# Attention scores by seven products: two partial sums accumulated in PSUM, with another order of the products and a later sum of the second queries

## The chip, the cores and the metric

One core of a Trainium2 chip runs the kernel. The metric is the device time of one execution in microseconds (us). TensorE (PE) multiplies, with its weight loads (PEld) beside it; VectorE (DVE), ScalarE (ACT) and GpSimd (POOL) work on tiles; SyncE (SP) issues nearly all DMAs, in the order in which they stand in its queue. Every engine takes its instructions in order.

## The reference

A layer with attention and a gated low-rank feed-forward part on the same normalized input, 2 sequences of 2048 tokens, width 2048, head width 512. Cut to what matters here:

```python
xn = layernorm(x)
q, k, v = split(xn @ Wqkv + bqkv)                 # each (2, 2048, 512)
attn = softmax((q @ k.T) / sqrt(512))             # (2, 2048, 2048)
out = x + (attn @ v) @ Wo + bo + ffn(xn)
```

The change lies in `q @ k.T`.

## The kernel before

**Number format.** Each operand is split into a high and a low part (`split_hi` on ScalarE, line 121, and `split_lo` on VectorE, line 124). A product of two operands is then three matmuls (low x high, high x low, high x high: `PASSES`), all added up in one PSUM bank.

**Stages.** First the projections of blocks of 512 tokens. For the last three of the four block pairs they run in `phase`, seven phases of seven items (six features and "V"), each item's weights fetched two pieces ahead by `fetch` (DMA at line 605, then the splits). A feature item is 24 matmuls of 512 columns; the V item, in two pieces, has matmuls of 264 columns. Beside each phase `beside` gives a list of small steps to be done by the other engines: among them `key_list`, `query_steps`, `query_load` and `query_split`. Then come the scores with the weighted sums, then the output projection.

**Scores.** The tokens are NB = 8 blocks of 512; two neighbouring blocks b0 and b1 are a pair (four pairs, `NPAIR`). The scores of a pair with two key tiles are a 2 x 2 block product, computed with seven products P1 to P7 instead of eight. Their operands are sums of blocks, made beforehand: key sums by `key_steps` (written to `kp_d`, line 853, loaded by `key_load`, line 945), query sums by `query_steps` (loads at line 905, additions at 908 to 911, stores to `qs_d` at line 915) and loaded by `query_load` (928). For one pair there are NKS = 8 key positions m; a pair and a position are called a unit here, so there are 32 units with 7 products each, 224 products, numbered g. One product is six matmuls of 512 columns (two halves of the head width, three passes).

`score(g)` (line 1089 is its matmul) does one product in the order `ORDER` and hands its bank on. `acc()` gives one of seven PSUM banks. P1 stays in its bank and P2 is added there by TensorE; everything else is added in SBUF by VectorE:

```python
if step == "P1":
    nc.scalar.copy(unit(b0, m)[:, 1, :], ps)
if step == "P6":
    tt(u[:, 1, :], u[:, 1, :], ps, ALU.add)
elif step == "P5":
    tt(unit(b1, m)[:, 1, :], u[:, 1, :], ps, ALU.add)
```

P3, P7 (twice) and P4 are additions of the same kind, so a unit has two copies on ScalarE (lines 1096 and 1101) and six additions on VectorE (1099 to 1113). `greatest` (1071, 1073) keeps the running maximum of the scores of a block, in VectorE.

**After the scores of a block.** `maxes` turns the running maximum into one maximum for each query, a chain of some ten small VectorE operations that ends in `mq` (1132). `spread` sends it to all partitions by one matmul (1142), and ScalarE copies it to `mbc` (1146). `soft(c)` does a chunk of 128 keys: VectorE subtracts (1158), ScalarE takes the exponential (1161), then the split into `ph`. `weigh(n)` multiplies the chunk by the values (`vt`, loaded from `v_d` by `load_v`, 1185), line 129.

**Order.** The main loop goes over g. After `score(g)`, with every second g, it loads the keys of two products eight ahead into a ring of five double tiles (`r_kt`), does the steps that `deal` has put at g, and from product 65 on some `weigh` calls of the pair before. So the first pair's 56 products run one after another, and between the products of pairs 1 to 3 there are six to nine matmuls of weighted sums. `maxes` of the pair's second block is called at the product n = 54 of its 56, `spread` of it at n = 1 of the next pair; the first block's follow at n = 2 and 4. The framework orders each engine's instructions by its own estimate, near to the order in the program, and puts a semaphore wait at every dependency; a DMA also waits for the one eight before it.

The query sums of pair 1 (`query_steps(1, mid(0, 1, 2, 3))`) are steps of the last projection phase, P4 of the last pair, in two halves `l0, s0, o0` and `l1, s1, o1`: load, sums, store. Their loads write the four tiles of one ring twice. The operands of pair 1 are loaded and split at n from -14 and -6 on.

Of the kernel before, what the change touches and what calls it, by code (L numbers as in the profile page):

```python
# [8 lines left out]
F32 = mybir.dt.float32  # L9
FR = mybir.dt.float32r  # L10
# [6 lines left out]
P = 128  # L17
# [16 lines left out]
def raw(ap):  # L34
    return ap.bitcast(F32)
# [27 lines left out]
def attn_ffn_kernel(ctx: ExitStack, tc, x, xT, wq, wv, wob, bqk, bv, bo, keysT, out):  # L63
# [26 lines left out]
    def mid(*js):  # L90
        return Ring(sb, *(f"h{j}" for j in js))
# [41 lines left out]
    def scratch(name, n):  # L133
# [7 lines left out]
        [dram.tile([P, 2, 2, 2, P], F32, name=f"kp_d{kb}_{n}") for n in range(7)] for kb in range(NB)  # L141
# [518 lines left out]
    def beside(j, ph):  # L660
# [49 lines left out]
        if more:  # L710
# [6 lines left out]
        k, (l0, s0, o0, l1, s1, o1) = key_list(7, 8, False), query_steps(1, mid(0, 1, 2, 3))  # L717
        return [], [
            [ql(0), ql(1), l0], [qp(0), ql(2), *k[:2]], [s0, qp(1), ql(3), *k[2:4]],
            [o0, qp(2), ql(4), l1, k[4]], [qp(3), ql(5), *k[5:7]],  # L720
            [qp(4), ql(6), s1, k[7], kl(0), kl(1)], [o1, kl(2), kl(3), qp(5), qp(6)],
# [110 lines left out]
    ORDER = ("P1", "P6", "P2", "P5", "P3", "P7", "P4")  # L832
# [3 lines left out]
    qop, kop = {}, {}  # L836

    def key_steps(kb, d):


        v = {}

        def load():
            for h in range(2):
                v[h] = ks["R"]([P, T], F32, "kr")
                nc.sync.dma_start(v[h], k_d[kb][h][:, d, :])

        def quad(a, h):
            return v[h].rearrange("p (m a k) -> p a m k", m=2, a=2)[:, a]

        def out():
            if "out" in v:
                nc.sync.dma_start(*v.pop("out"))

        def one(step):
            a00, a01, a10, a11 = (quad(a, h) for a in range(2) for h in range(2))
            tt = nc.vector.tensor_tensor
            out()
            src = {"P1": a00, "P2": a01, "P4": a11, "P5": a11, "P7": a10, "P6": a00, "P3": a01}[step]
            if step == "P5":  # L860
                tt(a11, a10, a11, ALU.add)
            if step == "P7":
                tt(a10, a00, a10, ALU.subtract)
            if step == "P6":
                tt(a00, a11, a00, ALU.subtract)
            if step == "P3":
                tt(a01, a01, a00, ALU.subtract)
            n = steps.index(step)
            if ks["n"] == 1 or n % 2 == 0:
                v["st"] = ks["st"]([P, ks["n"], 2, 2, P], FR, "kst")  # L870
            st = v["st"][:, n % ks["n"]]
            split_hi(st[:, :, 0, :], src)
            split_lo(st[:, :, 1, :], src, st[:, :, 0, :])
            v["out"] = kp_d[kb][ORDER.index(step)][:, :, :, d, :], raw(st)

        steps = ("P1", "P2", "P4", "P5", "P7", "P6", "P3")
        return load, [lambda step=step: one(step) for step in steps] + [out]
# [43 lines left out]
    def query_load(j, n):  # L921

        h, t = {"P1": (0, 0), "P2": (1, 0), "P3": (1, 1)}.get(ORDER[n], (0, 0))
        src = q_d[2 * j + t][h]
        if ORDER[n] in ("P4", "P5", "P6", "P7"):
            src = qs_d[j][{"P5": 0, "P6": 1, "P7": 2, "P4": 3}[ORDER[n]]]
        hi, lo = (r_qt([P, 2, T], FR, "qt") for k in range(2))
        nc.sync.dma_start(raw(lo), src)
        qop[j, n] = hi, lo

    def query_split(j, n):
        hi, lo = qop[j, n]
        split_hi(hi, raw(lo))
        split_lo(lo, raw(lo), hi)

    def key_load(i):

        if 2 * i >= NPAIR * NKS * 7:
            return
        t = r_kt([P, 2, 2, 2, P], FR, "kt")  # L940
        for o in range(2):
            st, n = divmod(2 * i + o, 7)
            j, m = divmod(st, NKS)
            kb = j // 2 * BPB + m // 2
            last["sp"] = nc.sync.dma_start(raw(t[:, o]), kp_d[kb][n][:, m % 2])
            kop[2 * i + o] = t[:, o]
# [92 lines left out]
    ks = {"R": mid(0, 1, 2, 3), "st": wide(0, 1, 2, 3, 4, 5), "n": 2}  # L1039
# [26 lines left out]
    def greatest(blk, m, a):  # L1066
        u = S[blk, m]
        if m == 0:
            if a:
                M[blk] = r_M([P, T], F32, "M")  # L1070
                nc.vector.tensor_tensor(M[blk], u[:, 0, :], u[:, 1, :], ALU.max)
        else:
            nc.vector.tensor_tensor(M[blk], M[blk], u[:, a, :], ALU.max)  # L1073

    bank = {}

    def score(g):

        st, n = divmod(g, 7)
        j, m = divmod(st, NKS)  # L1080
        b0, b1 = 2 * j, 2 * j + 1
        step = ORDER[n]
        more = step == "P2"
        ps = bank["P1"] if more else acc()
        bank[step] = ps
        k, q = kop.pop(g), qop[j, n]
        for d in range(2):
            for i, (a, c) in enumerate(PASSES):
                last["pe"] = nc.tensor.matmul(  # L1089
                    ps, k[:, a, d, :], q[c][:, d, :],  # L1090
                    start=not more and d == 0 and i == 0, stop=d == 1 and i == 2,
                    skip_group_check=more,
                )
        tt = nc.vector.tensor_tensor
        if step == "P1":
            nc.scalar.copy(unit(b0, m)[:, 1, :], ps)
        u, v = S[b0, m], S.get((b1, m))
        if step == "P6":
            tt(u[:, 1, :], u[:, 1, :], ps, ALU.add)
        elif step == "P2":  # L1100
            nc.scalar.copy(u[:, 0, :], ps)
        elif step == "P5":
            tt(unit(b1, m)[:, 1, :], u[:, 1, :], ps, ALU.add)
            greatest(b0, m, 0)
        elif step == "P3":
            tt(v[:, 0, :], v[:, 1, :], ps, ALU.add)
            greatest(b1, m, 0)
        elif step == "P7":
            tt(v[:, 1, :], v[:, 1, :], ps, ALU.add)
            tt(u[:, 1, :], u[:, 1, :], ps, ALU.add)  # L1110
            greatest(b1, m, 1)
        elif step == "P4":
            tt(u[:, 1, :], u[:, 1, :], ps, ALU.add)
            greatest(b0, m, 1)
# [33 lines left out]

    blocks = [2 * j + t for j in range(NPAIR) for t in (1, 0)]
# [294 lines left out]

    deal(NG1 + 2, [small_ring])
# [10 lines left out]
    for j in range(1, NPAIR):  # L1456
        deal(NG1 * j - 14, [lambda j=j: query_load(j, 0), lambda j=j: query_split(j, 0)], 5)
        for n in range(1, 7):
            deal(
                NG1 * j - 7 + n, [lambda j=j, n=n: query_load(j, n), lambda j=j, n=n: query_split(j, n)],  # L1460
                5 if j == 1 else 3,
            )
# [3 lines left out]
    for g in range(begin[-1]):  # L1466
# [8 lines left out]
        if j and j <= NPAIR:  # L1475
            if n == 2:
                maxes(2 * j - 2)
            if n in (1, 4):
                with behind("pe"):
                    spread(2 * j - 1 - n // 4)  # L1480
        if n == NG1 - 2 and j < NPAIR:
            maxes(2 * j + 1)
# [118 lines left out]
```

## Time and profile before

| | us |
|---|---|
| median of three runs | 2637.76 (2636.66 to 2639.0) |
| the profiled execution | 2636.59 |
| its span | 2634.8 |
| score matmuls, line 1089, first to last start | 1336.6 to 1912.3 |
| VectorE, additions of line 1106, each of 32 | 0.681 |
| ScalarE, copies of line 1096, each of 32 | 0.587 |
| ScalarE, casts of queries, 128x1024, each of 28 | 1.051 |
| VectorE, subtractions of queries, 128x1024, each of 28 | 1.252 |
| VectorE, subtractions at line 1158, each of 64 | 1.214 |
| ScalarE, exponentials, each of 64 | 1.061 |
| key loads, 256 KB, issue to landing, median of 224 | 5.2 |
| stores of key sums, 256 KB, median of 112 | 3.7 |

How to read a profile of this kind: a row names the source line, the engine, the operation and the tiles (written <- read), then busy time and the mean of one. A row of waits says which engine stood idle, for which engine's or DMA's work, how long in total, how often and the longest. The granted clock is the share of full clock that TensorE had in a window. The queue of SyncE shows when each DMA was issued and how long the issue stood; a DMA that waits holds all behind it. An idle engine matters only where TensorE waits for it, since TensorE is busy nearly all the time.

### The profile page before, as it was taken

What the parts mean: (1) busy time and instruction counts of PE and PEld (TensorE: products, weight loads), DVE (VectorE), ACT (ScalarE), POOL (GpSimd) and SP (SyncE); (2) the same over time, 40 slices, a digit from 0 to 9 for tenths busy, and PEclk for the clock granted to TensorE, in tenths of its full rate; (3) what the DMA queues carried; (4) which work ended last, traced back from release to release, by engine and by line L of the source; (5) the groups of instructions that cost most, each with busy time, mean ns of one, the idle gap of its engine ahead of it and who ended that gap; (6) DMA issues with size and microseconds to landing.
All of it is one profiled execution on the core that took longest, in us unless ns stands there. A gap on an engine that the chain in (4) does not pass through costs nothing. (4 is left out here: it accounts for less than half of the span.)

```text
span 2634.8 us, 34738 instructions
## 1 busy us (share of the span) xinstructions
PE 2596.4 (99%) x12689; PEld 2193.7 (83%) x12689; DVE 1987.5 (75%) x2827; ACT 859.2 (33%) x1249; POOL 521.7 (20%) x315
## 2 busy tenths in 40 slices
PE   8999999999999999999989999999999999999999
PEld 7889888888888888888777887878877888888887
DVE  6557639867878677776678979979798776797675
ACT  4323323323332333343323434334254222332221
POOL 1311520000000010000000000000000666566654
PEclk9999999999999999999999999999999999999999
DMA  6677775668446673587999798899788544565542
GB/s 234 220 251 268 275 267 188 210 212 277 152 137 226 211 272 126 181 252 224 296 309 311 247 330 283 263 328 321 259 283 293 180 165 164 181 220 177 173 163 101
DMA packets 348042, 608.09 MB, mean 231 GB/s; under 512 B 28456, under 2 KB 151392, under 8 KB 347872
## 3 DMA queue, kind: packets, MB, share of 16 engines
q1 hardware_dynamic: 334912, 575.99, 64.9%
q10 hardware_dynamic: 12960, 29.89, 3.4%
q8 instruction: 100, 1.64, 0.3%
q14 instruction: 70, 0.57, 0.1%
HBM read 450.42 MB, written 155.35 MB: 230 GB/s over the span
## 5 line engine op out<-in xcount | busy, mean ns | idle before, releaser
L129 PE MATMUL acc<-t,pw 128*128 128x512 f32 x3024 | 694.0, 390 | 0.8 <-DVE pw L124 0.8
L129 PEld LDWEIGHTS acc<-t,pw 128*128 128x128 f32 x3024 | 565.4, 188 | 118.8 <-DVE pw L124 1.6
L1363 PE MATMUL acc<-wb,s 128*128 128x512 f32 x2688 | 609.8, 389 | 0.3 <-ACT u L1375 0.3
L1363 PEld LDWEIGHTS acc<-wb,s 128*128 128x128 f32 x2688 | 504.4, 188 | 105.5 <-ACT u L1375 0.8
L1347 POOL TENSOR_TENSOR xo<-xo,bo_bc 128x512 f32<-128x512 f32 x128 | 207.8, 1630 | 900.5 <-DMA bo_bc<-in_bo 601.7
L129 PE MATMUL acc<-ph,vt 128*128 128x512 f32 x1536 | 379.0, 391 | 4.8 <-ACT ph L121 3.0
L129 PEld LDWEIGHTS acc<-ph,vt 128*128 128x128 f32 x1536 | 289.0, 189 | 67.5 <-ACT ph L121 3.3
L1089 PE MATMUL acc<-qt,kt 128*128 128x512 f32 x1344 | 336.7, 393 | 3.5 <-DMA kt<-kp_d 1.8
L1089 PEld LDWEIGHTS acc<-qt,kt 128*128 128x128 f32 x1344 | 254.6, 190 | 59.2 <-DVE qt L124 2.7
L121 ACT CAST pw<-pw 128x1024 fp32r<-128x1024 f32 (+1 forms) x168 | 177.7, 1058 | 338.1 <-PE acc L129 245.1
L124 DVE TENSOR_TENSOR pw<-pw 128x1024 fp32r<-128x1024 f32 (+1 forms) x168 | 213.6, 1272 | 79.2 <-ACT pw L121 77.6
L129 PE MATMUL acc<-xh,wh 128*128 128x512 f32 x1152 | 263.6, 390 | 0.0
L129 PE MATMUL acc<-pw,t 128*128 128x264 f32 x2016 | 249.3, 285 | 10.7 <-ACT pw L121 9.9
L129 PEld LDWEIGHTS acc<-pw,t 128*128 128x128 f32 x2016 | 247.8, 189 | 13.1 <-ACT pw L121 10.3
L129 PEld LDWEIGHTS acc<-xh,wh 128*128 128x128 f32 x1152 | 215.6, 188 | 44.9
L121 ACT CAST s<-xz 128x1024 fp32r<-128x1024 f32 x112 | 118.0, 1054 | 368.7 <-PE acc L1363 307.5
L124 DVE TENSOR_TENSOR s<-xz,s 128x1024 fp32r<-128x1024 f32 x112 | 173.1, 1548 | 40.1 <-ACT s L121 40.1
L124 DVE TENSOR_TENSOR wh<-wu,wh 128x512 fp32r<-128x512 f32 x96 | 80.9, 860 | 101.5 <-ACT wh L121 101.5
L518 POOL TENSOR_TENSOR zt<-zt,g 128x512 f32<-128x512 f32 x24 | 41.4, 1732 | 510.5 <-DMA g<-gd 312.3
L1352 DVE TENSOR_TENSOR xo<-xo,acc 128x512 f32<-128x512 f32 x128 | 86.8, 680 | 54.7 <-POOL xo L1393 24.0
L121 ACT CAST ph<-sp 128x512 fp32r<-128x512 f32 x128 | 78.8, 617 | 141.7 <-PE acc L129 136.2
L124 DVE TENSOR_TENSOR t<-xq,t 128x1024 fp32r<-128x1024 f32 x84 | 108.3, 1293 | 21.0 <-ACT t L121 20.5
(165 smaller groups left out, 2512.8 us busy)
## 6 DMA issues: line engine op xcount, KB each, us to landing
vt<-v_d SPq DMA_DIRECT2D x128, 512.0 KB, 4.9
kt<-kp_d SPq DMA_DIRECT2D x224, 256.0 KB, 5.2
pw<-sq_d SPq DMA_DIRECT2D x72, 512.0 KB, 4.1
xo<-in_x SPq DMA_DIRECT2D x128, 256.0 KB, 3.2
xz<-oz_d SPq DMA_DIRECT2D x64, 512.0 KB, 4.5
out_y<-xo SPq DMA_DIRECT2D x128, 256.0 KB, 2.6
kp_d<-kst SPq DMA_DIRECT2D x112, 256.0 KB, 3.7
pw<-in_wq SPq DMA_DIRECT2D x54, 512.0 KB, 4.2
```

What stands on the lines that cost most here:

```text
L121: return nc.scalar.copy(hi, src)
L124: return (eng or nc.vector).tensor_tensor(lo, src, raw(hi), ALU.subtract)
L129: last["pe"] = nc.tensor.matmul(ps, st(a_), mv(b_), start=first and n == 0, stop=end and n == 2)
L518: nc.gpsimd.tensor_tensor(zt, zt, gx[n], ALU.mult)
L1089: last["pe"] = nc.tensor.matmul(ps, k[:, a, d, :], q[c][:, d, :], start=not more and d == 0 and i == 0, stop=d == 1 and i == 2, skip_group ...
L1347: nc.gpsimd.tensor_tensor(xs, xs, bo_bc[q // (NB // 2 * NH), c], ALU.add)
L1352: nc.vector.tensor_tensor(xs, xs, ps, op)
L1363: nc.tensor.matmul(ps, st[a_][:, kk, sl], mv[b_], start=not more and kk == 0 and n == 0, stop=kk == ND - 1 and n == 2, skip_group_check=more,)
```

## The change

**The products of a unit.** The new order is `QO`: P1, P7, P2, P6, P4, P5, P3. The list `seq` puts P1 of the next unit ahead of P3 of this one, and in the first pair P7 too. After P1, ScalarE copies its bank to a second bank ("seed"); TensorE adds P6, P5 and P3 there, and ScalarE copies the sum out after each of the three. P2 is added in P1's own bank as before, P4 in P7's. A unit has five copies on ScalarE (the seed, P7, P2, P6, P3) and two additions on VectorE (at P4 and P5). The first three seeds are preceded by one matmul into their bank. In pair 0 the seed follows P1 at once; later it follows P3 of the unit before. `greatest` for the halves copied by ScalarE is called one product later (`later`).

**The order of blocks.** b0 is complete before b1, so `maxes`, `spread` and the weighted sums take the blocks in their natural order.

**Key sums.** The scratch tensors `kp_d` hold two products side by side, so that one store writes both; a load reads one product's part of each row. `out` issues the stores that have gathered. In the score stage the staging ring has three tiles where it had six (`wide(0, 1, 2)`).

**Query sums of pair 1.** They leave the last projection phase and are dealt to products 2, 6, 8, 12, 16 and 18 of the first pair, with a ring of their own (`r_qs`). Pair 1's first four operands are loaded to that ring at products 30 to 42 and split at 44 to 52; the other three are loaded at 53 to 55 and split four products later.

```diff
-        [dram.tile([P, 2, 2, 2, P], F32, name=f"kp_d{kb}_{n}") for n in range(7)] for kb in range(NB)
+        [dram.tile([P, 2, n, 2, 2, P], F32, name=f"kp_d{kb}_{s}") for s, n in enumerate((2, 2, 2, 1))]
+        for kb in range(NB)
@@ beside
-        k, (l0, s0, o0, l1, s1, o1) = key_list(7, 8, False), query_steps(1, mid(0, 1, 2, 3))
+        k = key_list(7, 8, False)
         return [], [
-            [ql(0), ql(1), l0], [qp(0), ql(2), *k[:2]], [s0, qp(1), ql(3), *k[2:4]],
-            [o0, qp(2), ql(4), l1, k[4]], [qp(3), ql(5), *k[5:7]],
-            [qp(4), ql(6), s1, k[7], kl(0), kl(1)], [o1, kl(2), kl(3), qp(5), qp(6)],
+            [ql(0), ql(1)], [qp(0), ql(2), *k[:2]], [qp(1), ql(3), *k[2:4]], [qp(2), ql(4), *k[4:6]],
+            [qp(3), ql(5), *k[6:]], [qp(4), ql(6), kl(0), kl(1)], [kl(2), kl(3), qp(5), qp(6)],
         ]
-    ORDER = ("P1", "P6", "P2", "P5", "P3", "P7", "P4")
+    QO = ("P1", "P7", "P2", "P6", "P4", "P5", "P3")
+    seq = [(0, "P1")]
+    for k in range(NPAIR * NKS):
+        seq += [(k, step) for step in QO[1:6]]
+        seq += [(k + 1, "P1")] * (k + 1 < NPAIR * NKS) + [(k, "P3")]
+
+    for k in range(NKS - 1):
+        g = seq.index((k, "P3"))
+        seq[g], seq[g + 1] = seq[g + 1], seq[g]
@@ key_steps
-            v["out"] = kp_d[kb][ORDER.index(step)][:, :, :, d, :], raw(st)
+            dst = kp_d[kb][n // 2][:, d]
+            if not two:
+                outs.append((dst[:, n % 2], raw(st)))
+            elif n % 2:
+                outs.append((dst, raw(v["st"])))
+            elif n == 6:
+                outs.append((dst[:, 0], raw(st)))
@@ query_split
-        hi, lo = qop[j, n]
-        split_hi(hi, raw(lo))
-        split_lo(lo, raw(lo), hi)
+        hl, at = qop[j, QO[n]]
+        hi, lo = hl or [r_qt([P, 2, T], FR, "qt") for k in range(2)]
+        split_hi(hi, at)
+        split_lo(lo, at, hi)
+        qop[j, QO[n]] = hi, lo
@@ key_load
-            last["sp"] = nc.sync.dma_start(raw(t[:, o]), kp_d[kb][n][:, m % 2])
+            last["sp"] = nc.sync.dma_start(raw(t[:, o]), kp_d[kb][n // 2][:, :, n % 2, m % 2])
@@ before score
-    ks = {"R": mid(0, 1, 2, 3), "st": wide(0, 1, 2, 3, 4, 5), "n": 2}
+    ks = {"R": mid(0, 1, 2, 3), "st": wide(0, 1, 2), "n": 2}
+    def seed(k):
+
+        b = bank["U"] = acc()
+        if k < 3:
+            nc.tensor.matmul(b, bank["k"], bank["q"], start=True, stop=True)
+        nc.scalar.copy(b, bank["P1"])
@@ score
+        more = step not in ("P1", "P7")
+        if step == "P6":
+            bank["U0"] = bank["U"]
+        name = {"P2": "P1", "P4": "P7", "P6": "U0", "P5": "U0", "P3": "U0"}.get(step, step)
...
+        if step == "P1":
+            bank["k"], bank["q"] = st[:, 0, 0, :], mv[0][:, 0, :]
+            if k < NKS:
+                seed(k)
+        elif step == "P7":
+            copy(unit(b1, m)[:, 1, :], ps)
+        elif step == "P2":
+            copy(unit(b0, m)[:, 0, :], ps)
+            later.append((b0, m, 0))
+        elif step == "P6":
+            copy(S[b0, m][:, 1, :], ps)
+        elif step == "P4":
+            tt(S[b0, m][:, 1, :], S[b0, m][:, 1, :], ps, ALU.add)
+            greatest(b0, m, 1)
+        elif step == "P5":
+            tt(S[b1, m][:, 1, :], S[b1, m][:, 1, :], ps, ALU.add)
+            greatest(b1, m, 1)
+        elif step == "P3":
+            copy(S[b1, m][:, 0, :], ps)
+            later.append((b1, m, 0))
+            if NKS <= k + 1 < NPAIR * NKS:
+                seed(k + 1)
-    blocks = [2 * j + t for j in range(NPAIR) for t in (1, 0)]
+    blocks = range(NB)
@@ main loop
+    r_qs = wide(3, 4, 5, 9)
+    for g, st in zip((2, 6, 8, 12, 16, 18), query_steps(1, r_qs)):
+        deal(g, [st])
...
+        for n in range(7):
+            g = NG1 * j - (14, 7, 5, 4, 3, 2, 1)[n]
+            if j > 1:
+                deal(g, [loads[n], splits[n]], (5, 3)[n > 0])
+            else:
+                g = (44, 49, 51, 52, 53, 54, 55)[n]
+                if n < 4:
+                    deal(30 + 4 * n, [lambda n=n: query_load(1, n, r_qs)])
+                else:
+                    deal(g, [loads[n]])
+                deal(g if n < 4 else g + 4, [splits[n]])
-                maxes(2 * j - 2)
+                maxes(2 * j - 1)
-                    spread(2 * j - 1 - n // 4)
+                    spread(2 * j - 2 + n // 4)
-            maxes(2 * j + 1)
+            maxes(2 * j)
```

## The prediction

> **What bounds the kernel now.** I read the busy shares first, then TensorE's waits, then short windows around each wait, then the DMA queue at the largest one. The busy shares:
>
> ```profile
> PE 2596.4 (99%) x12689; PEld 2193.7 (83%) x12689; DVE 1987.5 (75%) x2827; ACT 859.2 (33%) x1249; POOL 521.7 (20%) x315
> ```
>
> TensorE sets the time. The change removes no matmul, so only TensorE's lost time can be won: 38.4 us idle in the whole span, plus matmuls run at half clock after a gap. The waits (engine, what it waited for: us in total, times, longest), from the end of the projections to the end of attention:
>
> ```profile
> PE acc L129 <- ACT pw L121: 9.9, 1, 9.9
> PE misc L1142 <- DVE mq L1132: 4.8, 3, 2.4
> PE acc L129 <- ACT ph L121: 3.0, 1, 3.0
> PE acc L1089 <- DMA kt<-kp_d: 1.8, 1, 1.8
> PE acc L1089 <- DVE qt L124: 1.6, 1, 1.6
> ```
>
> Few, single waits, all at stage borders. Windows around them (TensorE's busy us, matmuls, granted clock, DMA share, GB/s) show what each costs with its half clock:
>
> ```profile
> 1346.50:1354.50 8.00, 6.19 (x21) 0.79 1.03 369
> 1418.50:1426.50 8.00, 6.34 (x19) 0.79 1.03 403
> 1427.50:1443.50 16.00, 12.90 (x47) 0.89 0.67 216
> 1586.50:1591.50 5.00, 3.34 (x14) 1.00 1.03 409
> 1755.50:1764.50 9.00, 6.59 (x22) 0.81 1.04 405
> 1916.50:1925.00 8.50, 7.70 (x32) 1.00 0.62 204
> 1800.00:1850.00 50.00, 50.00 (x222) 1.00 0.95 332
> ```
>
> In the chain of waits six 512-column matmuls take 1.36 us, 0.227 us each (the last row, without a stall, agrees). Lost time is length minus matmuls x 0.227:
> - B, 1347: 8 - 4.8 = 3.2 us, a key load came late
> - C, 1419: 8 - 4.3 = 3.7 us, pair 1's second query operand came late
> - D, 1428 to 1443: 16 - 10.7 = 5.3 us, the first weighted sum waits for its exponentials
> - E, 1587, 1756 and 1917: 1.8 + 4.0 + 1.2 = 7.0 us, `spread` waits for `maxes`
> - A, 1312 to 1327: 9.9 us idle, then 21 matmuls of 264 columns in 4.9 us where 78 take 9.5 us at full clock (0.12 each): 4.9 - 2.5 = 2.4. Together 12.3 us.
>
> The sum is 31.5 us. What holds A is in SyncE's queue (start us, us):
>
> ```profile
> 1296.03 0.61 SPq L605 DMA_DIRECT2D pw<-in_wq  x1
> ...
> 1306.93 2.06 SPq L915 DMA_DIRECT2D qs_d<-qs  x2
> ...
> 1309.08 5.09 SPq L905 DMA_DIRECT2D qs<-q_d  x4
> 1314.23 0.52 SPq L853 DMA_DIRECT2D kp_d<-kst  x1
> 1314.79 0.62 SPq L605 DMA_DIRECT2D pw<-in_wv  x1
> ```
>
> The last V weights (`in_wv`) stand behind pair 1's query sums: four loads, four stores that wait for VectorE, and four loads into the same ring that wait for those stores. 18.8 us pass between two weight loads.
>
> **Part 1, query sums of pair 1 leave the last projection phase.** Their 16 DMAs and 8 additions go to the first score pair. In the changed program's built order five DMAs, not seventeen, stand between these two weight loads, none into a ring that waits for a store. What is late next there? The split of those weights on ScalarE waits for TensorE to finish with item 3 (about 1301, items take 5.4 us); load 3.6 us, cast 1.08, subtraction 1.35 put it near 1305, and TensorE needs it at 1311.9. So A goes whole: **12.3 us**. B too: the loads for products 8 and 9 now stand ahead of the `v_d` stores that held them: **3.2 us**.
>
> What it costs: the moved DMAs are 256 KB each, 4.2 MB, of which 1 MB was already issued after 1334. The first pair (1336.5 to 1424) moved 332 GB/s x 87.5 us = 29 MB at a share of 0.98. Without its stalls it lasts about 80 us: 32 MB in 80 us is 400 GB/s, and the most seen in a window is 409. At nothing if the ten-product key ring (13.6 us of lead, 5.2 us of it a landing) covers it; if it doesn't, 32 MB at about 370 GB/s takes 86 us, a loss of 6. Larger stores help (part 4). I take **-2.5 us**, nearer the covered end.
>
> **Part 2, sums in PSUM.** A unit (one pair, one key position, seven products; 32 of them) had six VectorE additions of 679 ns and two ScalarE copies of 587 ns. It gets two additions and five copies: VectorE -4 x 32 x 0.68 = -87 us, ScalarE +3 x 32 x 0.587 = +56 us. In 1443 to 1912 VectorE is busy 409 of 469 us, ScalarE 170: 87% and 36% become about 73% and 45%. Neither becomes the bound on its average.
>
> The copy from PSUM to PSUM has no row here. The nearest, ScalarE PSUM to SBUF (L1096), takes 587 ns; below, a cast of half the size takes 406, above, the SBUF-to-SBUF cast of this size 620. I take 587; the ends change ScalarE by -6 to +1 us and TensorE not at all while the copy is covered.
>
> New waits of TensorE: P2 waits until the seed has read P1's bank, P5 until P6's sum has been copied out of the shared bank. In pair 0 the seed has two products, 2.7 us, for 0.6 us of copy; P6's copy has one, 1.36 us. In pairs 1 to 3 weighted sums stand between, so both have over 4 us. Queued ahead on ScalarE are casts of `kst`, which wait for stores, and exponentials, which wait for VectorE:
>
> ```profile
> ACT sp L1161 <- DVE sp L1158: 32.9, 28, 5.6
> ACT kst L121 <- DMA kp_d<-kst: 22.9, 16, 3.4
> ```
>
> A wait of mean 1.2 or 1.4 us fits into 4 us, the longest not quite; in pair 0 a wait of 1.4 us ahead of P6's copy does not fit. I take **-1 us** in pair 0 (two or three such meetings) and **-1.5 us** later. Three dummy products to set up the banks: 3 x 0.227 = **-0.7 us**. Here a rule speaks against the change. The Trainium skill (PSUM — Partial Sum Buffer, "The four PSUM rules") says that writes of ScalarE don't touch the bits that decide whether a matmul adds or overwrites, and asks that a non-zero seed go through TensorE. By it every seed would need a matmul, 32 x 0.227 = 7.3 us; the program issues three and relies on the bits that earlier products left. No row shows the bits; the built order counts three, so the sum has 0.7.
>
> **Part 3, shorter VectorE queue before `spread`.** Around 1580 to 1590 VectorE has no gap: the small operations of `maxes` stand among additions, splits and exponent subtractions. In the built order, between the last addition that waits for TensorE and `mq` there are now some 5 to 8 us of VectorE work at the durations of its rows, against about 9 us from P5's end to `spread` in pairs 1 to 3 (three products and their weighted sums) and 6.8 us before pair 1 (five products). So E mostly goes: **5 of 7.0 us**. D: its chain is mbc copy 0.59, subtraction 1.21, exponential 1.06, split 0.62 and hand-overs, near 5 us, and `spread` now stands 6 products (8.2 us) ahead of the first weighted sum, formerly 4. But the seed of unit 9 is queued on ScalarE behind that exponential, and P2 needs it: **2.5 of 5.3**.
>
> C: four query loads of pair 1 are issued 17 to 25 products before use, into a staging ring; three still wait for an operand slot that products 52 to 54 free. A query load lands in 6.8 to 7.9 us, the splits take 1.05 and 1.25: the first of the three is ready some 9.4 us after its issue, and its use comes 7 products, 9.5 us, after it. The first `mq` now stands behind its split. **1.5 of 3.7**.
>
> What a stall costs: the Trainium skill (TensorE: Matmul & The Clock Gate, "Why this matters for your kernels") warns of idle gaps above some 3 us. Here the row decides: the 1.8 us wait at 1347 was followed by a clock of 0.79 in its window, the 1.7 us wait at 1587 by 1.00. By the rule B would be worth 1.8, C 1.6 and the 2.4 us at 1756 no more than themselves, and A to E near 24 us; by the rows 31.5. I use the rows, and price new stalls with the same surcharge.
>
> **Part 4, layout of key sums.** Stores of pairs of products: 112 become 79 (33 fewer DMAs on SyncE), in 4 KB or 2 KB rows where there were 512 B pieces; loads (224) fall from 2 KB to 1 KB rows. In the packets of this trace 512 B take 27 ns, 2 KB 84, 4 KB 159 and 1056 B 47: stores gain about 0.2 us each (16 engines), loads lose about 0.06. DMA work changes by -22 + 14 = -8 us in all, hidden behind TensorE: nothing, beyond what part 1 counts.
>
> **Sum:** 12.3 + 3.2 + 1.5 + 2.5 + 5 - 2.5 - 1 - 1.5 - 0.7 = 18.8 us. The profiled execution took 2636.6 us (span 2634.8), so 2617.8; the median of the runs lies 1.2 us higher. I predict **2619 us**.
>
> **Rivals.**
> 1. *The borders refill (0.2).* A and B go, but query operands, seeds and `maxes` still meet after product 55, so C, D, E return as other waits, and first-pair DMA costs its 6 us: 2637.8 - 15.5 + 6 + 3.2 of ScalarE and dummies = 2631. For it: ScalarE waits 32 us for query loads already. Against: VectorE has a sixth less to do.
> 2. *ScalarE becomes a wait in every unit (0.1), slower.* Place: P6's copy ahead of P5, or the seed ahead of P2, behind a blocked cast. Price: 1.5 us a unit with clock, 48 us, less the 24.5 won: about 2661. It decides from 0.8 us a unit (24.5 / 32). For it: the single product of cover in pair 0. Against: over 4 us of cover in the other 24 units.
> 3. *The change does more (0.15).* All of A to E goes and nothing is added: 2637.8 - 31.5 + 0.7 = 2607.
> 4. *The V weights stay late (0.05)*, behind ScalarE's casts: no change, 2635.
>
> **Numbers.** The forecast's own case has 0.5, 2612 to 2627. The range 2605 to 2632 takes in rivals 1 and 3 and leaves out 2 and 4. No change means within 0.2%, 5.3 us, what this kernel's measurement can tell: faster 0.83, same 0.07 (rival 4 and the bad end of 1), slower 0.10.
>
> **What would show it.** No wait on `pw` before the scores; key loads of the first pair within a few us of need, DMA share near 1; TensorE's waits on ScalarE's copies below 3 us in all; waits on `mq` below 2; ScalarE copies at 587 ns; VectorE 87 us less. The prediction is wrong if TensorE waits on the seed or P6's copy in most units, or on key loads again and again in the first pair.

## The result, and the profile after

| | before | after |
|---|---|---|
| median of 17 runs each, us | 2638.4 (2629.4 to 2647.6) | 2631.6 (2620.4 to 2635.3) |
| ratio, 95% interval | | 0.9969 (0.9957 to 0.9981) |
| profiled span, us | 2634.8 | 2628.2 |

The change makes the kernel 0.3% faster: 6.8 us by the medians, 8.2 us by the ratio (5.0 to 11.3). The forecast was 18.8. The sign is as predicted, and the time is inside the range, but less than half of the gain came. The forecast's own case (2612 to 2627) is missed; 2631 is the price of rival 1, by another road, as will be seen.

First the busy shares of the changed kernel, then TensorE's waits (waits: engine, line, what it waited for, us in total, times, longest):

```profile
PE 2592.6 (99%) x12692; PEld 2186.3 (83%) x12692; DVE 1919.4 (73%) x2698; ACT 909.8 (35%) x1345; POOL 516.1 (20%) x315
```

```profile
PE acc L1129 <- ACT acc L1112: 7.4, 2, 7.2
PE acc L1129 <- ACT sp L1155: 5.0, 5, 1.6
...
PE acc L129 <- DVE ot L1255: 2.5, 2, 2.2
...
PE acc L1129 <- DMA kt<-kp_d: 1.9, 3, 0.8
PE misc L1186 <- DVE mq L1176: 1.8, 3, 1.0
PE acc L129 <- DVE ph L124: 1.7, 2, 1.2
```

The waits of before are gone or small: none for the V weights (`ACT pw`, 9.9), none for `qt` (1.6), `mq` 1.8 where it was 4.8. In their place stand two waits for ScalarE that before did not have. L1112 is the seed, and one wait of 7.2 us is the **first** seed of all. L1155 is ScalarE's copy of the last sum, after P3.

To place them I use one measure for all kernels below: the lost time of TensorE, which is the distance between the starts of neighbouring matmuls less what the same matmul takes at full clock (0.227 us for 512 columns), summed over the gaps. It includes half clock. The stages are cut by the work, not by the time.

| lost us, one profiled execution | last V item to product 9 | products 10 to 51 | 52 to 67 | 68 to 223 | after the last product |
|---|---|---|---|---|---|
| before | 16.3 | 0.2 | 9.7 | 7.7 | 4.8 |
| after | 9.9 | 3.4 | 1.9 | 15.9 | 2.3 |

Before the last V item each profile has 23 to 31 us more, whichever kernel it is of; so single executions differ there by up to 8 us, and only the stages behind it are compared. The stalls at the second border (C and D) went nearly whole and the end is better. But the first border, with the products up to 51, won only 3.2 us of the 15.5 of A and B, and pairs 1 to 3 lost 8 us more than before.

**The first seed.** This is ScalarE's timeline in the changed kernel where TensorE stands still (start us, us, work, count, and in brackets the idle time before it and what ended it):

```profile
1313.02 1.05 ACT L121 CAST qt<-qt 128x1024 fp32r<-128x1024 f32 x1 [1.53 <-DMA qt<-q_d]
1323.63 0.41 ACT L121 CAST kst<-kr 128x256 fp32r<-128x256 f32 x1 [9.56 <-DMA kr<-k_d]
1326.04 0.71 ACT L121 CAST kst<-kr 128x256 fp32r<-128x256 f32 x2 [2.00 <-DMA kr<-k_d]
1327.73 0.94 ACT L121 CAST kst<-kr 128x256 fp32r<-128x256 f32 x2 [0.98 <-DVE kr L877]
1328.96 0.41 ACT L121 CAST kst<-kr 128x256 fp32r<-128x256 f32 x1 [0.29 <-DVE kr L881]
1329.69 1.06 ACT L121 CAST vs<-vs 128x264 fp32r<-128x264 f32 x3 [0.32 <-DVE vs L289]
1330.65 0.57 ACT L1112 COPY acc<-acc 128x512 f32<-128x512 f32 x1
```

The seed takes 0.57 us. It stands behind six casts of the key sums of step 8 (block 4; the expectation of the first run below says block 8), and the first of these waits 9.56 us for a key load. That load was issued late, as SyncE's queue shows (start us, us):

```profile
1317.95 0.33 SPq L163 DMA_DIRECT2D oz_d<-zt  x1
1318.32 1.19 SPq L973 DMA_DIRECT2D kt<-kp_d  x2
1319.56 1.07 SPq L858 DMA_DIRECT2D kr<-k_d  x2
```

The scores now start at 1320.9, not at 1336.6; P1 is done, the key operands have come, but P2 may not be added to P1's bank until the seed has read it. From 1323.6 TensorE waits, and then runs at half clock:

```profile
1323.00:1336.50 13.50, 6.27 (x17) 4.67 (x16) 6.53 (x18) 5.35 (x13) 0.00 (x0) 0.62 0.67 225
```

(A window: length, busy us and count of PE, PEld, DVE, ACT, POOL, granted clock, DMA share, GB/s.) Nothing needs those six casts soon. Their place on the engine is all that makes them matter.

**The bank.** The five waits for L1155 are at P7 of a unit in pairs 1 to 3. The longest, on ScalarE and on TensorE:

```profile
1616.58 0.57 ACT L1112 COPY acc<-acc 128x512 f32<-128x512 f32 x1 [1.26 <-PE acc L1129]
1620.50 0.40 ACT L121 CAST kst<-kr 128x256 fp32r<-128x256 f32 x1 [3.34 <-DMA kp_d<-kst]
1620.81 0.61 ACT L121 CAST ph<-sp 128x512 fp32r<-128x512 f32 x1
1621.33 0.40 ACT L121 CAST kst<-kr 128x256 fp32r<-128x256 f32 x1
1621.63 0.58 ACT L1155 COPY sp<-acc 128x512 f32<-128x512 f32 x1
```

```profile
1619.11 1.52 PE L129 MATMUL acc<-ph,vt 128*128 128x512 f32 x6
1622.26 1.67 PE L1129 MATMUL acc<-qt,kt 128*128 128x512 f32 x6 [1.64 <-ACT sp L1155]
```

P3's copy is held by a cast that waits for a store. But P7 doesn't read that copy: it starts a new sum in an empty bank. What it waits for is the bank. The seed of the next unit (1616.58) stands ahead of P3's copy here, though the program has it behind; in the order in which banks are taken, it got the one that P4 had left; with P1's, the old second bank and four banks of weighted sums all seven are in use, and P7 gets the one that this late copy empties.

### The profile page after: what moved, and what is told of

Read it like the earlier page. It is cut to its first block, busy times and chain, and to the rows that moved or that the text cites. A ratio compares the mean times of both kernels' runs of the same rounds, so it can differ in the third digit from the quotient of the medians.

```text
span 2628.2 us, 34501 instructions
## 1 busy us (share of the span) xinstructions
PE 2592.6 (99%) x12692; PEld 2186.3 (83%) x12692; DVE 1919.4 (73%) x2698; ACT 909.8 (35%) x1345; POOL 516.1 (20%) x315
## 3 DMA queue, kind: packets, MB, share of 16 engines
q8 instruction: 100, 1.64, 0.3%
## 5 line engine op out<-in xcount | busy, mean ns | idle before, releaser
L121 ACT CAST t<-xq 128x1024 fp32r<-128x1024 f32 x84 | 88.3, 1052 | 103.5 <-PE acc L129 44.8
```

Source lines behind the costliest of these rows:

```text
L121: return nc.scalar.copy(hi, src)
```

## The experiments

**The first seed's place (three runs).** The first run changes an order on ScalarE and nothing else:

```diff
-        nc.scalar.copy(b, bank["P1"])
+        c = nc.scalar.copy(b, bank["P1"])
+        last.setdefault("seed", c)
@@ main loop, the dealt steps
-            with behind("sp"):
+            with behind("sp", *(["seed"] if 5 <= g < 13 else [])):
                 st()
```

> The changed kernel with one edit of order: ScalarE's casts of the key sums at products 5 to 12 are placed behind the first copy from P1's bank to the second bank (the first seed); nothing is added or taken away. My theory: the 7.4 us that TensorE waits for the first seed at 1323.6, and the 2.5 us at half clock behind it, come from the place of that copy in ScalarE's queue, behind casts that wait for key loads. Then the wait goes (under 1 us left) and the kernel is 8 to 10 us faster than the changed one, 15 to 18 us faster than the kernel before. Rival: the key loads themselves are late after the last projection phase, and TensorE meets them a few products later (key sums of block 8, a wait for kt); then the wait on the seed goes but 5 us or more of it come back as waits on DMA in the first ten products, and the gain on the changed kernel is under 4 us.

Measured: 2623.35 us, ratio 0.9937 (0.9919 to 0.9955), 17 us faster than before. Against the changed kernel the two ratios give 0.9968, or 8.4 us, with about 5.8 to each side. The same place on ScalarE:

```profile
1324.10 1.15 ACT L121 CAST vs<-vs 128x264 fp32r<-128x264 f32 x3 [7.18 <-DVE vs L289]
1326.28 0.57 ACT L1112 COPY acc<-acc 128x512 f32<-128x512 f32 x1 [1.02 <-PE acc L1111]
```

The seed now waits for TensorE, as it should, and the wait for it is 0.2 us in the whole kernel. Lost time at the first border falls from 9.9 to 2.7, and the next stage stays (3.4 and 3.6): the late key loads cost TensorE nothing more. So the trace rules the rival out; the time alone, with its interval, would not. Of the 2.7 us that are left, 2.2 are one wait at P3, by the same pattern on another engine. P3 adds to the bank that VectorE has to read after P5, and VectorE stands behind the first query sums, which wait for their load:

```profile
PE acc L1130 <- DVE sp L1153: 2.1, 1, 2.1
```

```profile
1335.33 0.69 DVE L928 TENSOR_TENSOR qs<-qs 128x512 f32<-128x512 f32 x1 [3.52 <-DMA qs<-q_d]
```

Does the stall belong to the seed, or to the earlier arrival of TensorE? The kernel before with later query sums alone has no seed:

```diff
-        k, (l0, s0, o0, l1, s1, o1) = key_list(7, 8, False), query_steps(1, mid(0, 1, 2, 3))
+        k = key_list(7, 8, False)
...
-    ks = {"R": mid(0, 1, 2, 3), "st": wide(0, 1, 2, 3, 4, 5), "n": 2}
+    ks = {"R": mid(0, 1, 2, 3), "st": wide(0, 1, 2), "n": 2}
...
+    r_qs = wide(3, 4, 5, 9)
+    for g, st in zip((2, 6, 8, 12, 16, 18), query_steps(1, r_qs)):
+        deal(g, [st])
```

> The kernel before with one part of the change alone: the query sums of pair 1 are taken out of the last projection phase and dealt to products 2 to 18 of the first pair, with a ring of their own (and three staging tiles for key sums in place of six). Products, PSUM and the order of the blocks are those of before. My theory: this part alone is worth the wait for the last V weights, 12.3 us, less 2 us or so of first-pair DMA, and here no seed waits: 9 to 13 us faster than the kernel before, so as fast as the changed kernel or a few us faster. Rival: the DMA moved into the first pair costs what the phase gains, since the DMA engines are at a share of 0.98 there; then the wait for pw is gone, waits for kt and qt in the first pair grow by 6 us or more, and the gain is under 5 us.

Measured: 2635.77 us, ratio 0.9983 (0.9974 to 0.9993), some 4.5 us, less than the theory's 9 to 13. The gain is as the rival had it, the reason is not. Its TensorE waits, and ScalarE at that place:

```profile
PE acc L1088 <- ACT sp L1095: 10.0, 2, 9.6
```

```profile
1332.21 0.40 ACT L121 CAST kst<-kr 128x256 fp32r<-128x256 f32 x1 [11.76 <-DMA kr<-k_d]
...
1338.23 0.58 ACT L1095 COPY sp<-acc 128x512 f32<-128x512 f32 x1
```

The wait for `pw` is gone, and 9.6 us of wait for ScalarE's copy of the first P1 have come (P2 is added in that bank here too), behind the same casts. So it isn't the new arithmetic that made this stall. Freeing the V weights brings TensorE to the scores before the key loads, in either kernel, and in both the framework put the casts ahead of the copy. Next, the same kernel with its first P1 copy ahead of those casts (the edit of the first run, at line 1095):

> The kernel before with the query sums of pair 1 taken to the first pair, as in the run before this one, and besides ScalarE's casts of the key sums at products 5 to 12 placed behind its copy of the first P1. My theory now: what the later query sums win at the V weights is lost again at the first units, because TensorE arrives there earlier than the key loads and ScalarE's copy of P1 stands behind a cast that waits for them (9.6 us of wait in that run). With the copy ahead of the casts this wait falls below 1.5 us, and the kernel is 8 to 11 us faster than without the new place, so 11 to 15 us faster than the kernel before. Rival: the key loads are late for TensorE too; then the wait comes back within the first ten products as a wait for kt or for VectorE, and the time stays within 3 us of the run without the new place (about 5 us faster than the kernel before).

Measured: 2631.79 us, ratio 0.9971 (0.9959 to 0.9983): 7.6 us. Lost time at the first border goes from 13.1 to 3.4, as the theory had it, and from product 10 to 51 it rises from 2.9 to 8.7, as the rival had it. Its waits, and VectorE's largest wait between 1318 and 1362 (busy us, mean ns, idle us before it and the releaser; two instructions, 4.75 and 2.36 us of waiting):

```profile
PE acc L1088 <- DMA kt<-kp_d: 4.9, 4, 1.8
...
PE acc L1088 <- DVE qs L907: 3.0, 1, 3.0
```

```profile
L907 DVE TENSOR_TENSOR qs<-qs 128x512 f32<-128x512 f32 x2 | 1.4, 692 | 7.1 <-DMA qs<-q_d 7.1
```

VectorE stands 7.1 us in two waits for the loads of the query sums, and TensorE runs into it (3.0 us). With the sums in PSUM the like costs 2.1 us in the first run. Whether the later sums pay more with the sums in PSUM is not shown: here, with the casts moved, they are worth 7.6 us, and in the changed kernel, by the comparison below, 7.

**The V weights: later sums or fewer stores (three runs).** The changed kernel with the query sums put back into the last projection phase, `beside` as before the change and the new dealing left out:

> The changed kernel with the query sums of pair 1 back in the last projection phase (the part with the order of the products and the sums in PSUM stays). My theory: the later query sums alone end the wait for the last V weights, worth 12.3 us, so with them undone the wait for pw (9 to 11 us) is back. The seed's wait of 7.4 us may shrink, since the key loads are then issued while TensorE stands still; so the kernel is 4 to 12 us slower than the changed one, about the time of the kernel before (2632 to 2642). Rival: the order of the queue is free to differ and the weights come in time anyway because the new layout of the key sums has fewer stores there; then no wait for pw is seen and the time is within 2 us of the changed kernel.

Measured: 2627.15 us, ratio 0.9947 (0.9929 to 0.9964). This is not 4 to 12 us slower than the changed kernel but 6 us faster by the two ratios (interval 0.3 to 11). The wait for `pw` is back at 3.9 us, where the theory said 9 to 11, since the last V weights are issued at 1309.96, 5 us earlier than before (1314.79 there).

And here the framework put the first seed ahead of the casts by itself. Up to product 51 this run lost 11.4 us and the changed kernel 13.3: with that obstacle the later sums, as they stand in the change, win nothing there. The rest of the difference lies in pairs 1 to 3 (12.1 against 15.9), 3 us of it at one place, 1511, which is looked at below. Is it the stores that let the weights out? The kernel before with the new layout of the key sums alone (scratch, `out`, load, and the index order of the score matmul):

> The kernel before with the new layout of the key sums alone: one store for two products, loads that read a part of each row. Products, query sums, PSUM and rings are those of before. In the prediction this part cost and won nothing. With the query sums left in their place in the changed kernel the wait at the V weights was 3.9 us where it is 9.9 in the kernel before, and their loads were issued 5 us earlier. Theory: fewer stores in SyncE's queue let those weights out earlier; then the wait for pw shrinks here too, to 3 to 6 us, and the kernel is 5 to 9 us faster than before. Rival: the earlier issue came with the new order of the products (which operands are loaded there), not with the stores; then the wait for pw stays at 9 to 10 us and the time within 2 us of before.

Measured: 2638.53 us, ratio 0.9997 (0.9987 to 1.0006). The wait for `pw` fell from 9.9 to 5.8 as the theory said, but the 5 to 9 us did not come; the interval leaves room for 3.4 at most. The last loads of the two kinds of weights stand 18.8 us apart in the kernel before. In the run with the sums put back, and then in this one:

```profile
1299.53 0.42 SPq L606 DMA_DIRECT2D pw<-in_wq  x1
1309.96 0.43 SPq L606 DMA_DIRECT2D pw<-in_wv  x1
```

```profile
1304.71 0.42 SPq L606 DMA_DIRECT2D pw<-in_wq  x1
1315.05 0.43 SPq L606 DMA_DIRECT2D pw<-in_wv  x1
```

That is 10.4 and 10.3 us, so the layout alone brings them closer. Its 1315.05 looks no earlier than the 1314.79 of before only because TensorE, late from earlier stages in this execution, comes to these weights at 1316.8 and not at 1311.9. Against its arrival they are issued 1.7 us ahead here, 2.6 us ahead with the sums put back, and 2.9 us late before. The layout thus takes a part of A by itself, which part 1 had counted whole for the later sums. It is a small part of the time: the first stage lost 13.9 against 16.3, and "nothing" was not far off.

Last, the same question with both obstacles of the changed kernel removed (the edits of the first run and of the last one below, and the query sums put back):

> The run before this one (casts behind the first seed, second bank taken after P7's) with the query sums of pair 1 back in the last projection phase: what the later query sums are worth once nothing else stands in their way. The prediction's own terms make it 12.3 + 3.2 - 2.5 = 13 us, so 2630. My theory: less, since the new layout of the key sums had already let the V weights out some 5 us earlier; in the earlier run with the sums put back, the lost time of TensorE from the last V item to the end of the first pair was 11.5 us against 6.4 to 6.6 with them moved, so 5 us: 2622, 14 to 17 us faster than the kernel before. Rival: the sums moved into the first pair cost there what they win, and the time is within 2 us of the run before this one (2615 to 2619).

Measured: 2626.29 us, ratio 0.9944 (0.9927 to 0.9960), against 2616.97 and 0.9918 with the sums moved. The later sums are worth 7 us by the ratios (1 to 13) and 6.4 in lost time over the first two stages (12.5 against 6.1). The prediction's terms made it 13.

**The bank (three runs).** First I tried to free the second bank one product earlier, by P3 ahead of the next unit's P1 from the second pair on (and the seed right behind P1):

```diff
-        seq += [(k + 1, "P1")] * (k + 1 < NPAIR * NKS) + [(k, "P3")]
+        nxt_ = [(k + 1, "P1")] * (k + 1 < NPAIR * NKS)
+        seq += nxt_ + [(k, "P3")] if k + 1 < NKS else [(k, "P3")] + nxt_
```

> The changed kernel with one edit of order, from the second pair on: P3 of a unit stands before P1 of the next (in the changed kernel it stands after), so the second bank's last sum is copied out one product earlier, and the seed follows its own P1 at once. My theory: in pairs 1 to 3 the scores hold three PSUM banks and the weighted sums four, which is all seven, so P7 of a unit waits until ScalarE has emptied the bank of the unit before (waits of TensorE for the copy at P3, 5.0 us in 5 waits, with half clock some 6 us). Then these waits fall below 1.5 us in all and the kernel is 4 to 6 us faster than the changed one. Rival: they come from blocked casts and exponentials ahead of the copy on ScalarE, whatever the bank; then the same total moves to P2 or P7 (a wait for the copy, 4 us or more) and the time stays within 2 us of the changed kernel.

Measured: 2635.34 us, ratio 0.9973 (0.9964 to 0.9983), the same as the changed kernel. The waits for P3's copy are gone, but the edit brought a dependency of its own: P3 now follows P5 in the same bank, and waits until VectorE has read P5's sum (L1152; of the three sums in the second bank ScalarE copies out only P6's and P3's).

```profile
PE acc L1130 <- DVE sp L1152: 8.3, 10, 1.5
PE acc L1130 <- ACT acc L1113: 5.0, 1, 5.0
```

So the run decides nothing on the bank. It shows what P1 between P5 and P3 is for. Then an eighth bank for the ring, on top of the first run's edit:

```diff
-        return psum.tile([P, T], F32, name="acc", tag="acc", bufs=7)
+        return psum.tile([P, T], F32, name="acc", tag="acc", bufs=8)
...
-        return psum.tile(shape or [P, T], F32, name="misc", tag="misc", bufs=1)
+        t = psum.tile([P, T], F32, name="misc", tag="acc", bufs=8)
```

> The changed kernel with ScalarE's casts behind the first seed, and with one ring of eight PSUM banks in place of seven and one: the small transposes and the spread of the maxima take their bank from the same ring. My theory: P7 of a unit waits for the bank of the unit before, which ScalarE's copy after P3 sets free (3.7 us in 5 waits in the run with the casts moved, with half clock 4.5 us), since three score banks and four banks of weighted sums fill all seven. With an eighth bank these waits fall below 1 us and the kernel is 3 to 5 us faster than that run, near 2619. Rival: the copy is late for its own reason, so the wait moves to the next user of that bank; then over 3 us of waits for ScalarE's copies stay, at P7 or at another product, and the time is the same within 2 us.

Measured: 2627.21 us, ratio 0.9957 (0.9944 to 0.9970), some 5 us slower than the run without the eighth bank (by the two intervals, from 11 us slower to as fast), where 3 to 5 us faster was expected. The waits for P3's copy are gone here too. But the framework ordered other instructions anew, and `mq` became late:

```profile
PE misc L1192 <- DVE mq L1182: 10.8, 6, 3.6
...
PE acc L1135 <- ACT sp L1153: 1.4, 1, 1.4
...
PE acc L1135 <- ACT sp L1148: 1.0, 1, 1.0
```

Two edits had each moved more than the bank. The third, on top of the first run's edit, changes who gets which bank: the seed takes its bank after P7 has taken one. It changes one thing more than was expected. In the built order of the first run the seed stood ahead of P3's copy in 22 of the 24 later units; here it stands behind it from the third of them on:

```diff
         elif step == "P7":
+            if k >= NKS:
+                seed(k)
             copy(unit(b1, m)[:, 1, :], ps)
@@ at P3
-            if NKS <= k + 1 < NPAIR * NKS:
-                seed(k + 1)
```

> The changed kernel with ScalarE's casts behind the first seed, and in pairs 1 to 3 with the second bank of a unit taken after the bank of its P7 and no longer at P3 of the unit before. The order of instructions on ScalarE stays P3's copy, seed, P7's copy; what differs is which bank goes to whom: P7 gets the bank that P4 of the unit before left two products ago, the seed gets the one that the copy after P3 has just left, which stands ahead of it on the same engine. My theory: P7's waits for the copy after P3 (3.7 us in 5 waits in the run with the casts moved, 4.5 us with half clock) come from this assignment, three score banks in use for four tiles alive at that place; so they fall below 1 us, nothing takes their place, and the kernel is 3 to 5 us faster than that run, 20 us or so faster than the kernel before. Rival: ScalarE is late there for its own reasons; then P2 or P6 waits for the seed instead, 3 us or more in all, and the time stays within 2 us.

Measured: 2616.97 us, ratio 0.9918 (0.9901 to 0.9934), 21 us faster than before and the fastest of all. Against the first run that is 5 us (from 11.5 to -1.4 by the intervals), which is not settled. The trace settles the cause of the waits. No wait of TensorE for P3's copy is left, though ScalarE is late here too. Its timeline at the place of the 1.64 us wait shown above, and P7 on TensorE:

```profile
1608.37 0.41 ACT L121 CAST kst<-kr 128x256 fp32r<-128x256 f32 x1 [4.99 <-DMA kp_d<-kst]
1608.69 0.62 ACT L121 CAST ph<-sp 128x512 fp32r<-128x512 f32 x1
1609.21 0.40 ACT L121 CAST kst<-kr 128x256 fp32r<-128x256 f32 x1
1609.52 0.58 ACT L1158 COPY sp<-acc 128x512 f32<-128x512 f32 x1
1610.12 0.57 ACT L1112 COPY acc<-acc 128x512 f32<-128x512 f32 x1
1610.69 0.59 ACT L1145 COPY sp<-acc 128x512 f32<-128x512 f32 x1
```

```profile
1609.13 1.52 PE L1130 MATMUL acc<-qt,kt 128*128 128x512 f32 x6
```

A cast stands 4.99 us behind a store, and the copy of P3's sum begins 1.6 us after P3's end (1.7 in the first run, 2.4 in the changed kernel). P7 starts at 1609.13, before that copy has even begun: it already had a bank. At the next unit the copy is later still, 2.4 us after P3's end, and P7 does not wait either. A late copy alone, then, does not stop TensorE; the assignment of banks made it a wait.

What the bank is worth in time is less than the forecast of 3 to 5 us. Between products 52 and 223 the lost time falls from 12.6 to 11.1 us, though the five waits had cost 4.5 there; other waits have come, among them two at P3 for VectorE's reading of P5's sum in pairs 2 and 3 (0.7 us each; the third of this row is the one of the first pair):

```profile
PE acc L1130 <- DVE sp L1155: 3.2, 3, 1.7
```

Of the 4.4 us between the two profiled executions, some 2.4 lie before the last V item, where the edit does nothing.

Lost time of all runs, by the same stages:

| | last V item to product 9 | 10 to 51 | 52 to 67 | 68 to 223 | after |
|---|---|---|---|---|---|
| casts behind the first seed | 2.7 | 3.6 | 1.9 | 10.7 | 1.5 |
| and the seed's bank after P7's | 4.0 | 2.1 | 1.0 | 10.1 | 1.8 |
| these two, query sums back | 12.4 | 0.1 | 1.0 | 10.8 | 1.6 |
| casts behind, eight banks | 3.7 | 3.5 | 5.3 | 16.6 | 1.2 |
| after, query sums back | 11.0 | 0.4 | 1.8 | 12.1 | 2.1 |
| after, P3 first | 7.7 | 3.5 | 1.9 | 17.5 | 3.0 |
| before, later sums | 13.1 | 2.9 | 11.9 | 6.2 | 5.1 |
| before, later sums, casts behind | 3.4 | 8.7 | 10.8 | 9.8 | 6.2 |
| before, new stores | 13.9 | 0.1 | 9.7 | 10.3 | 5.2 |

## Why the prediction was off

**The step that failed** is the end of part 1: "So A goes whole: 12.3 us". The forecast asked what is late next at the V weights, and found nothing. It did not ask what is late next at the scores, where TensorE then arrives 15.7 us earlier. The term for ScalarE stood elsewhere in the sum, as "-1 us in pair 0", worked out from the mean wait of its casts in the kernel before, 1.2 or 1.4 us. Measured, the first stage lost 9.9 us, nearly all of it at the first seed. The prediction looked for casts that wait for stores (mean 1.4 us, longest 3.4). The same view of waits has the casts that wait for key loads in the next line, mean 2.5 us:

```profile
ACT kst L121 <- DMA kr<-k_d: 22.3, 9, 6.3
```

ScalarE's timeline of the kernel before has the very cast, and this longest wait:

```profile
1338.16 0.59 ACT L1096 COPY sp<-acc 128x512 f32<-128x512 f32 x1 [1.02 <-PE acc L1089]
...
1348.05 0.40 ACT L121 CAST kst<-kr 128x256 fp32r<-128x256 f32 x1 [6.26 <-DMA kr<-k_d]
```

There it stands behind the first copy of P1 and holds up nothing. In the built order of the changed kernel six of these casts stand ahead of the first seed. Row and order together would have given the price; a mean over the whole kernel could not. An edit that only takes this stall away gives back 8.4 us (some 3 to 14), 7.2 of them at this place by the lost time.

**A second term was mis-sized**, the "-1.5 later" for ScalarE in pairs 1 to 3. By stages, the lost time won against the kernel before (the forecast's terms put to their stages, E's 5 us shared out over its three places):

| us won | forecast | the changed kernel | with the casts behind the first seed |
|---|---|---|---|
| last V item to product 51 | 11.3 | 3.2 | 10.2 |
| products 52 to 67 | 4.0 | 7.8 | 7.8 |
| products 68 to 223 | 2.6 | -8.2 | -3.0 |
| after the last product | 0.9 | 2.5 | 3.3 |
| sum | 18.8 | 5.3 | 18.3 |

With the casts moved the first border comes out as forecast, and the gain on before is 17 us. That its sum meets the 18.8 is luck: pairs 1 to 3 are 5.6 us short, and the second border and the end pay 6.2 more than forecast.

Point by point:
- **A and B.** The waits named are gone. What replaced them is above. Later sums are worth 7 us (1 to 13) once nothing else stands in the way, not 13; the new layout already has a part of A.
- **First-pair DMA, -2.5.** The waits for `kt` are 1.9 us and the stage lost 3.4 where it had 0.2. About right.
- **C and D, 1.5 and 2.5.** More came: the stage fell from 9.7 to 1.9. The seed of unit 9, named as what keeps half of D, kept 0.4 at most.
- **E, 5 of 7.0.** Waits for `mq` fell from 4.8 to 1.8. Right.
- **Later ScalarE, -1.5.** Too small, for the list of new waits had P2 and P5 in it but not P7. P7's cover isn't 4 us: between P3's end and P7 stands one group of weighted sums, 1.5 us. The five waits of 5.0 us in all cost 6.3 us of lost time, at a granted clock of 1.00: what is added is some 0.3 us at the start of the matmuls after each gap, not the half clock that the expectations of the runs put there. Another 4 us went at 1511, where a weighted sum waits for the bank of an output tile (`ot`) whose ring waits for a store, and about 2 us at 1763 at `ph`. These last two were not tried by themselves; at the first the other runs with the new sums lost between nothing and 1.8 us, so it may be a matter of the moment.
- **ScalarE and VectorE.** 96 more copies took ScalarE 51 us more (56 predicted). VectorE has 68 us less, not 87; the reason was not traced. Three dummy matmuls stand in the trace, not 32, so 0.7 and not 7.3 was the term to use.
- **Rival 1** had the size, by luck, from other terms: it let C, D and E return, and these went. **Rival 2** is out: TensorE waits seven times for ScalarE's seeds and copies, not in each unit. **Rival 4** is out.
- **The clock.** The 7.2 us wait had 0.62 in its window, as rows and rule would both have it. The 2.2 us wait at 1511 had 0.74, for the rows and against the rule. But the surcharge put on new stalls of 1 to 2 us did not come: the waits for P3's copy had 1.00.

## What to carry to other kernels

When a stall is removed, follow the bottleneck engine to the next place where it needs another engine, and read that engine's queue in program order there: an instruction of 0.6 us waits as long as the slowest thing ahead of it, needed or not. Count buffers as well as data: a matmul that starts a new sum waits for whoever last read its bank, and the order in which tiles are taken decides who that is. If a reordered edit moves other instructions too, read its trace before its time.

## What the runs showed of the hardware

The same gap does not always cost the same clock. A gap here runs from the start of one matmul to the start of the next, less 0.227 us; the profile's own waits are some 0.16 us shorter. In these traces single gaps of up to 1.8 us kept full clock, and those from 2.6 us on were followed by half clock. Between them both happen at the same size. A gap of 1.97 us was followed by half clock at 1347 in the kernel before (0.79 in the window shown in the prediction) and not at 1338 in the kernel before with later sums and the casts moved (1.00). Two gaps of 2.46 us lie in one execution, that with eight banks, at 1418 and 1590; the last three figures of each window are granted clock, DMA share and GB/s:

```profile
1417.00:1425.00 8.00, 4.23 (x17) 2.72 (x16) 7.81 (x17) 3.46 (x6) 0.00 (x0) 1.00 1.06 369
1589.00:1597.00 8.00, 5.70 (x18) 4.07 (x17) 7.82 (x15) 3.27 (x5) 0.00 (x0) 0.79 0.61 194
```

Further ones with half clock behind them are 1.90 us at 1420 in the kernel before, 2.14 at 1343 in the changed kernel with the sums put back and 2.35 at 1511 in the changed kernel; without it, 2.24 at 1336 in the first run, 2.38 at 1760 in the kernel before with later sums, and 1.90 twice in the fastest. Small gaps close together can do it too: 0.61, 0.72 and 0.93 us within 3 us were followed by half clock at 1423 in the kernel before with later sums (0.83 from 1418 to 1428), and the same three gaps were not at 1413 with the casts moved (1.00 from 1411 to 1421). So a stall of that size can't be priced to better than the 1.2 to 1.9 us that half clock added in the others; what decides between the two was not found.

ScalarE's copy from one PSUM bank to another, which the trace of before did not have, takes 0.572 us, about as long as a copy to SBUF (0.582 to 0.585).
